# A graph network's edge loop: which engine fetches a sender's row, and the update's inputs

## The chip, the core and the metric

The kernel runs on one core of a Trainium2 chip. The core's engines run side by side, each on its own queue of instructions in the order given: TensorE (PE, with its weight loads PEld) multiplies matrices, VectorE (DVE) and ScalarE (ACT) work elementwise, GpSimd (POOL) issues the indirect gathers here, and SyncE (SP) issues most plain DMAs. ACT can issue DMAs too. The metric is the device time of one execution in microseconds. The kernel before takes 5600.84 us, the median of 12 runs (5595.15 to 5619.77).

## What is computed

There are 12,500 nodes of 64 features and 412,500 edges, sorted by receiver, each with 32 features. With h the layer norm of x, cut off at zero, each edge makes a message and an attention logit from its sender's row, its receiver's row and its own features. The softmax runs over all edges. The weighted messages are summed by receiver, and a small network makes the update that is added to x.

```python
h = jnp.maximum(_layernorm(x, axis=-1), 0.0)
msg_in = concat([h[src], h[dst], edge])            # 64 + 64 + 32
messages = swish(msg_in @ W1 + b1) @ W2 + b2
att = softmax(swish(msg_in @ Wa1 + ba1) @ Wa2 + ba2, axis=0)
aggregated = segment_sum(messages * att, dst)
x = x + swish(concat([h, aggregated]) @ Wu1 + bu1) @ Wu2 + bu2
```

Everything is float32.

## The kernel before

**The node stage.** The nodes are padded to 98 blocks of 128. Their normalized features h are made once, and kept transposed in SBUF as `hT`, two nodes to a column. Two tables are written to DRAM: `ts_d`, a row of 128 numbers for each node as a sender (h times the sender's part of Wa1 and W1), and `tr_d`, the same for the receiver with the biases. `hT_d` is a copy of `hT` in DRAM.

**The edge loop.** An edge tile is 125 edges (`EP`), one edge to a partition, and a group is 8 tiles (`K`); there are 413 groups (`NG`). `load(g)` brings a group's operands, two groups ahead of the group's own step (`AHEAD`). The senders' rows come from `ts_d` by indirect gathers on POOL, one for each tile, into one of the 7 buffers of the pool `gather` (L511 to L515). The gathers have 125 rows in even tiles and 126 in odd ones (`WIDE`); the last row of the 126 is not used. The receivers of a group lie in a window of 40 consecutive nodes (`W`), as two halves of 32, since the edges are sorted. Two DMAs on SP load the window's rows of `tr_d` (L534), at an address that SP reads from `base_sb`. Comparisons on DVE (L538) make a selection matrix from the edges' receivers, and one matrix product for each two tiles (L542) selects the receivers' rows and adds the edges' own features in one go. There are three window buffers (`WINS`), so a window's load waits for the product three groups before.

`begin(g)` adds the gathered rows to that product on DVE (L553) and takes tanh on ACT (L556). `end(g)` makes the messages and logits on DVE (L566 to L577); after its last read a gather buffer is free. Every fourth group the maximum is renewed and the exponentials are taken (L607, L610). `sum_up(g)`, some groups later, weighs the messages: DVE makes weight matrices (L620), PE sums by node (L626) and projects (L637), ACT copies between the two (L632), and DVE adds into `sums` at an address read from registers (L655, L658).

**Columns.** One group in three (`chosen`, `EVERY` and `PHASE`) doesn't gather its eighth tile. ACT copies the 125 senders' columns out of `hT` instead, one copy each at an address from a register (L484), with an address instruction ahead of each copy. The copies are issued in six lots of 24, 24, 24, 12, 24 and 17 (`SLOTS`), two lots at each step of the loop, one after `begin` and one after `end` (`burst`). The numbers of the senders come by a DMA on SP (`numbers`, L458), DVE turns them into columns (`places`, L467 to L473), a comparison picks the half (L547), and a product with `stack` adds the rows (L548); in `begin` a copy (L555) takes the place of the eighth add.

**The update's inputs.** Between the groups 17 and 120, the inputs of the update at the end are laid out in DRAM. `tile_bias`, in two steps for each of 13 node tiles, loads `hT_d` back from DRAM (L329), multiplies, copies on ACT (L348) and writes `bq_d`. `tile_rest` loads x, adds a bias on DVE and writes `xb_d`, all in one step. After the loop, 13 node tiles are finished from these.

**What sets the order.** `pin` keeps instructions in the program's order on their engine; a tile framework adds the waits that data and buffers need. DMAs of SP go round eight semaphores, and each waits until the one eight before it has landed. POOL's queue holds the gathers alone, so it runs ahead of the loop as far as the buffers allow.

Of the kernel before, what the change touches and what calls it, by code (L numbers as in the profile page):

```python
# [72 lines left out]

EVERY = 3
PHASE = 1
SLOTS = (((0, 24), (24, 24)), ((48, 24), (72, 12)), ((84, 24), (108, 17)))
ROUND = 12582912.0
WIDE = 126
EPS = 1e-5
# [4 lines left out]
PARTS = [("pair", 4 * C), ("we", C), ("bias", C), ("wu2h", 2 * D), ("wa2", U), ("bu2", D), ("w_bu", U),  # L84
         ("w2b", U), ("wu1a", U), ("wu2", D), ("ba2", 1)]
HALVED = 4
# [4 lines left out]
def gnn_kernel(ctx: ExitStack, tc: tile.TileContext, n_edges, x, src, src_row, dst, dst_row, first, edge,  # L91
# [33 lines left out]
    we, bias, wa2, bu2_r, ba2_c = (part[k] for k in ("we", "bias", "wa2", "bu2", "ba2"))  # L125
    w_bu = part["w_bu"][:D + 1]
    w2b = part["w2b"][:S1]
    wu1a, wu2 = part["wu1a"][:U], part["wu2"][:U]
# [32 lines left out]
    gather = ctx.enter_context(tc.tile_pool(name="gather", bufs=7))  # L161


    with tc.tile_pool(name="node1", bufs=1) as node1, \
# [40 lines left out]

        eps = node1.tile([P, 1], F32, name="eps")
        nc.vector.memset(eps, EPS)
# [127 lines left out]
def tile_bias(tc, c, first, v, work, ps, bus):  # L335

    nc = tc.nc
    m = min(NC, v["NB"] - c)
    if first:
        bus[c] = work.tile([U, P * NC], F32, name="bu", bufs=1)[:, :P * m]  # L340
    elif m <= 4:
        return
    i = 0 if first else 4
    n = min(4, m - i)
    pb = node_bias(tc, c + i, v, work, ps).rearrange("u b (h p) -> u h p b", h=2)
    to = bus[c].rearrange("u (h k p b) -> u k h p b", h=2, k=2, b=m // 2)
    for k in range(i // (m // 2), (i + n) // (m // 2)):
        nc.scalar.copy(to[:, k], pb[:, :, :, k * m // 2 - i:(k + 1) * m // 2 - i])  # L348
    if i + n == m:
        for h in range(2):  # L350
            nc.sync.dma_start(v["bq_d"][c // NC, h * U:(h + 1) * U, :P // 2 * m],
                              bus[c][:, h * P // 2 * m:(h + 1) * P // 2 * m])

# [5 lines left out]

def tile_rest(tc, c, v, work):  # L360

    nc = tc.nc
    n = min(NC, v["NB"] - c)
    xt = work.tile([P, 4, P], F32, name="hb").rearrange("p a b -> p (a b)")[:, :n * D]
    for k in range(2):
        nc.sync.dma_start(
            xt[k * P // 2:(k + 1) * P // 2].rearrange("p (h b d) -> p h b d", h=2, d=D),
            halves(v["x"], c, n, k, v["NB"]))
    xv = xt.rearrange("p (b d) -> p b d", d=D)
    nc.vector.tensor_tensor(xv, xv, v["bu2_r"][:, None, :].to_broadcast([P, n, D]), ALU.add)  # L370
    nc.sync.dma_start(v["xb_d"][c // NC, :, :n * D], xt)


def one_pass(tc, n_edges, v):
    nc = tc.nc
    NB, T, NG, NP, NT = (v[k] for k in ("NB", "T", "NG", "NP", "NT"))
    ident, iota_w, bj, dloc, src_full, base_sb, real, unreal, far, wrong = (
        v[k] for k in ("ident", "iota_w", "bj", "dloc", "src_full", "base_sb", "real", "unreal",
                       "far", "wrong"))
# [12 lines left out]
    with ExitStack() as ctx:  # L392
# [5 lines left out]
        stand = keep.tile([P, NH + 2 * W], F32, name="stand")  # L398
        base_lo = keep.tile([1, NG + 1], I32, name="base_lo")
        base_hi = keep.tile([1, NG + 1], I32, name="base_hi")  # L400
        nc.vector.memset(base_lo, 0)
# [34 lines left out]
        with tc.tile_pool(name="work2", bufs=2) as work2, \  # L436
                tc.tile_pool(name="small", bufs=3) as small, \
                tc.tile_pool(name="pre_ps", bufs=AHEAD + 1, space=PSUM) as pre_ps, \
                tc.tile_pool(name="one_ps", bufs=1, space=PSUM) as one_ps:
            pes, gss, lgs, ps_, psums, sps, pps, ees, mts, nums, cols = ({} for _ in range(11))  # L440

# [9 lines left out]

            chosen = {g for g in range(8, NG - 12) if g % EVERY == PHASE}

            def numbers(g):
                if g in chosen:
                    e = (g * K + K - 1) * EP
                    n = nums[g] = small.tile([P, EP], I32, name="num", bufs=2)
                    nc.sync.dma_start(n, bass.AP(tensor=v["src_row"].tensor,  # L458
                                                 offset=v["src_row"][:, e:].offset, ap=[[0, P], [1, EP]]))

            def places(g):
                if g not in chosen:
                    return
                n = nums[g]
                near = small.tile([1, EP], F32, name="near", bufs=1)
                to = small.tile([1, EP], I32, name="to", bufs=2)
                pin(nc.vector.tensor_scalar(to, n[0:1], 1, None, op0=ALU.logical_shift_right))  # L467
                m = NB // 2
                pin(nc.vector.tensor_scalar(near, to, 1.0 / m, 0.5 / m - 0.5, op0=ALU.mult, op1=ALU.add))
                pin(nc.vector.tensor_scalar(near, near, ROUND, None, op0=ALU.add))  # L470
                pin(nc.vector.tensor_scalar(near, near, ROUND, float(1 - m * P), op0=ALU.subtract, op1=ALU.mult))
                pin(nc.vector.scalar_tensor_tensor(to, to, float(P), near, op0=ALU.mult, op1=ALU.add))
                pin(nc.vector.tensor_scalar(n, n, 1, None, op0=ALU.bitwise_and))  # L473
                cols[g] = small.tile([P, EP], F32, name="cols", bufs=2), to

# [10 lines left out]
            def burst(g, k):  # L486
                for i in range(EVERY):
                    columns(g + 3 + i, *SLOTS[EVERY - 1 - i][k])

            at_sp, at_lo, at_hi, bus = {}, {}, {}, {}  # L490

# [4 lines left out]
            def registers(g, engine, at, base=base_sb, top=NP - 1):  # L496
# [4 lines left out]
                for i in range(n):  # L501
                    at[g + i] = regs[i]

            def load(g):

                t = g * K
                if g % NQ == 0:
                    registers(g, ENG.SP, at_sp)
                full = gather.tile([P, K, C], F32, name="gs")
                gs = gss[g] = full[:EP]  # L510
                for j in range(K - (g in chosen)):  # L511
                    rows = WIDE if j % 2 == 1 else EP
                    nc.gpsimd.indirect_dma_start(  # L513
                        out=full[:rows, j, :], out_offset=None, in_=ts_d[:, :],
                        in_offset=bass.IndirectOffsetOnAxis(ap=src_full[:rows, t + j:t + j + 1], axis=0))  # L515
                if g % NQ == 0:
# [16 lines left out]
                for r in range(2):  # L533
                    nc.sync.dma_start(win[r * R:(r + 1) * R, :, r, :],  # L534
                                      tr_w[bass.ds(at_sp[g], R), :, :])
                for h in range(2):
                    e = slice(h * E2 // 2, (h + 1) * E2 // 2)
                    pin(nc.vector.tensor_scalar(eo[:WR, e], db[:, e], bj[g // NQ % 2 * WR:(g // NQ % 2 + 1) * WR, g, h:h + 1], None,  # L538
                                                op0=ALU.is_equal))
                pe = pes[g] = pre_ps.tile([P, K, C], F32, name="pe")[:EP]  # L540
                for q in range(H):
                    pin(nc.tensor.matmul(pe[:, 2 * q:2 * q + 2, :], eo[:, q * EP:(q + 1) * EP],  # L542
                                         win[:, q // 2, :, :], start=True,
                                         stop=q < H - 1 or g not in chosen))
                if g in chosen:
# [4 lines left out]
            def begin(g):  # L550

                n = K - (g in chosen)
                pin(nc.vector.tensor_tensor(gss[g][:, :n, :], pes[g][:, :n, :], gss[g][:, :n, :], ALU.add))  # L553
                if n < K:
                    pin(nc.vector.tensor_copy(gss[g][:, n, :], pes[g][:, n, :]))  # L555
                pin(nc.scalar.activation(pes[g], gss[g], AF.Tanh))  # L556
# [161 lines left out]
            for g in range(NG):  # L718
# [18 lines left out]
                if g + AHEAD < NG:  # L737
                    load(g + AHEAD)
                numbers(g + EVERY + 4)
                places(g + EVERY + 3)  # L740
                if more:
# [20 lines left out]
                if g == min(40, NG):  # L762
                    pin(nc.vector.tensor_reduce(far[:, 1:2], dloc, AX.X, ALU.min, negate=True))
                if g == min(44, NG):

# [3 lines left out]
                    pin(nc.tensor.transpose(worst_ps, worst.to_broadcast([EP, EP]), ident[:EP, :EP]))  # L769
                if g == min(45, NG):  # L770
                    pin(nc.vector.tensor_reduce(worst, worst_ps, AX.X, ALU.max))
                    pin(nc.vector.tensor_scalar(wrong, worst, 0.0, None, op0=ALU.is_gt))
                if g >= 16 and g // 8 - 2 < NT:
                    c = (g // 8 - 2) * NC
                    if g % 8 in (1, 5):
                        tile_bias(tc, c, g % 8 == 1, v, work2, one_ps, bus)
                    elif g % 8 == 3:
                        tile_rest(tc, c, v, work2)

# [273 lines left out]
def _laid_out(w):  # L1053
# [16 lines left out]
    part["ba2"][:] = w["ba2"]  # L1070
    part["w_bu"][:D + 1] = np.concatenate([w["Wu1"][:D], w["bu1"][None]])
    part["w2b"][:S1] = np.concatenate([w["W2"], w["b2"][None]])
    part["wu1a"][:U] = w["Wu1"][D:]
# [42 lines left out]
```

## Time and profile before

| | |
|---|---|
| median of 12 runs | 5600.84 us |
| the profiled execution, its time | 5631.02 us |
| its span, first to last instruction | 5629.3 us |
| mean granted TensorE clock | 0.597 |
| first gather starts, last ends | 52.1 us, 5522.7 us |
| first tanh, last tanh (L556) | 101.2 us, 5577.8 us |
| busy: DVE, ACT, POOL, PE | 59%, 44%, 63%, 46% |

The profile is one execution. A group of instructions is given as: line, engine, operation, output and inputs, count, then busy time in us and mean duration of one in ns, then the idle time of the engine just before them and what ended most of it. "issue" stands for idle time in which the engine waited for nothing that the profile shows. Register and address instructions and the issuing of DMAs are not counted as busy. A name with a q (SPq) means the engine's sequencer. In the windows view each engine has its busy time and the number of instructions in that stretch. In the timeline a row is: start, duration, engine, line, operation, count, and in brackets the idle time before it and what ended it.

### The profile page before, as it was taken

How to read it: one execution, taken by the hardware profiler on the slowest of the kernel's cores; microseconds unless marked ns; L12 is line 12 of the kernel's file. 1: busy time of each engine (PE TensorE's matmuls, PEld its weight loads, DVE VectorE, ACT ScalarE, POOL GpSimd, SP SyncE). 2: the span in 40 equal slices, each digit the busy share in tenths (PEclk: the TensorE clock that was granted, in tenths of full speed). 3: DMA queues.
4: the chain of work that ended last, by engine and by line, in shares of the span. 5: the costliest groups of instructions: out<-in, count | busy, mean ns of one | idle time of the engine just before them, and what ended most of it. 6: DMA issues, size and time to landing. Idle time of an engine off the chain costs nothing. (4 is left out here: it accounts for less than half of the span.)

```text
span 5629.3 us, 81803 instructions
## 1 busy us (share of the span) xinstructions
PE 2567.6 (46%) x11509; PEld 2001.9 (36%) x11509; DVE 3347.3 (59%) x9768; ACT 2485.4 (44%) x17651; POOL 3538.5 (63%) x3198
## 2 busy tenths in 40 slices
PE   5244544444444444444444444444444444444446
PEld 4233333333333333333333333333333333333335
DVE  6365656656656555555555555565656555555557
ACT  3344444444444444444444444444444444444422
POOL 4666666666666666666666666666666666666662
PEclk8565656666656555555555565566565555555556
DMA  7233333233232222222222222222222222222232
GB/s 227 61 73 70 76 78 76 69 80 77 71 71 65 62 63 68 58 66 61 65 65 63 64 67 59 65 62 66 66 62 64 68 58 65 60 66 65 62 82 68
DMA packets 335625, 398.57 MB, mean 71 GB/s; under 512 B 170293, under 2 KB 266088, under 8 KB 334690
## 3 DMA queue, kind: packets, MB, share of 16 engines
q0 software_dynamic: 205168, 205.98, 15.6%
q1 hardware_dynamic: 128530, 177.64, 13.1%
q10 hardware_dynamic: 1376, 9.67, 0.4%
q14 instruction: 457, 3.74, 0.2%
q8 instruction: 94, 1.54, 0.1%
HBM read 365.34 MB, written 25.72 MB: 69 GB/s over the span
## 5 line engine op out<-in xcount | busy, mean ns | idle before, releaser
L513 POOL DMA_INDIRECT gs<-ts_d,src_sb x3173 | 3521.2, 1110 | 1999.1 <-issue 1886.4
L484 ACT COPY cols<-hT 128x1 f32 x16375 | 1900.4, 188 | 2523.3 <-issue 2440.6
L542 PE MATMUL pe<-wins,eo 128*125 128x256 f32 x3304 | 1507.6, 634 | 863.9 <-DVE lg L577 257.3
L542 PEld LDWEIGHTS pe<-wins,eo 128*125 128x125 f32 x3304 | 1001.1, 319 | 1195.5 <-DVE lg L577 296.8
L637 PE MATMUL mt<-ss,w2u 65*128 65x40 f32 x826 | 225.1, 369 | 1305.4 <-DVE gm L603 583.1
L620 DVE TENSOR_SCALAR wt<-iota_w,dloc,p 125x40 f32<-125x40 f32 x3304 | 748.8, 333 | 1.6
L626 PE MATMUL sp<-wt,acts 125*65 125x40 f32 x6608 | 719.4, 286 | 17.1 <-issue 14.1
L637 PEld LDWEIGHTS mt<-ss,w2u 65*128 65x128 f32 x826 | 208.8, 296 | 1454.1 <-issue 822.2
L626 PEld LDWEIGHTS sp<-wt,acts 125*65 125x65 f32 x6608 | 682.2, 205 | 23.9 <-issue 17.0
L566 DVE SCALAR_TENSOR_TENSOR acts<-pe,gs 125x512 f32<-125x512 f32 x413 | 284.6, 689 | 560.2 <-ACT pe L556 438.8
L553 DVE TENSOR_TENSOR gs<-pe,gs 125x1024 f32<-125x1024 f32 (+1 forms) x413 | 486.5, 1178 | 182.6 <-remote 119.2
L556 ACT ACTIVATE pe<-gs 125x1024 f32<-125x1024 f32 x413 | 422.6, 1023 | 344.5 <-DMA gs<-ts_d,src_sb 101.8
L655 DVE TENSOR_TENSOR sums<-sums,mt 64x40 f32 x606 | 115.7, 191 | 511.5 <-remote 482.6
L596 PE MATMUL mt<-ident,mx 125*128 125x125 f32 x110 | 48.1, 437 | 591.8 <-DVE sums L655 251.7
L538 DVE TENSOR_SCALAR eo<-dbs,bj 64x250 f32<-64x250 int32 x826 | 289.7, 378 | 18.2 <-DMA dbs<-in_dst_row_dram 8.7
L574 DVE TENSOR_TENSOR pe<-pe,w_all 125x512 f32<-125x512 f32 x413 | 288.8, 699 | 13.4
L572 DVE SCALAR_TENSOR_TENSOR pe<-pe,gs 125x512 f32<-125x512 f32 x413 | 286.9, 695 | 9.2
L577 DVE TENSOR_REDUCE lg<-pe 125x8 f32<-125x512 f32 x413 | 283.8, 687 | 9.5
L547 DVE SCALAR_TENSOR_TENSOR cols<-num,half,cols 128x125 f32<-128x125 int32 x131 | 45.7, 349 | 367.0 <-ACT cols L484 298.8
L596 PEld LDWEIGHTS mt<-ident,mx 125*128 125x128 f32 x110 | 20.0, 182 | 603.3 <-remote 434.0
L691 DVE SCALAR_TENSOR_TENSOR total<-total,scale,psum 125x1 f32<-125x1 f32 x110 | 23.5, 214 | 297.1 <-ACT p L610 274.8
L548 PE MATMUL pe<-stack,cols 128*125 128x128 f32 x262 | 78.3, 393 | 208.9 <-DVE cols L547 122.1
(125 smaller groups left out, 1207.9 us busy)
## 6 DMA issues: line engine op xcount, KB each, us to landing
eo<-in_edge_dram SPq DMA_DIRECT2D x103, 500.0 KB
dbs<-in_dst_row_dram SPq DMA_DIRECT2D x206, 250.0 KB
gs<-ts_d,src_sb POOLq DMA_INDIRECT x3173
wins<-tr_d SPq DMA_DIRECT2D x826, 32.0 KB
num<-in_src_row_dram SPq DMA_DIRECT2D x131, 62.5 KB
ts_d<-ts SPq DMA_DIRECT2D x5, 896.0 KB
tr_d<-tr ACTq DMA_DIRECT2D x5, 896.0 KB
hT_d<-hT ACTq DMA_DIRECT2D x1, 3136.0 KB
```

What stands on the lines that cost most here:

```text
L484: pin(nc.scalar.copy(to[:, first + i:first + i + 1], hT[:, bass.ds(regs[i], 1)]))
L513: nc.gpsimd.indirect_dma_start(out=full[:rows, j, :], out_offset=None, in_=ts_d[:, :], in_offset=bass.IndirectOffsetOnAxis(ap=src_full[:ro ...
L538: pin(nc.vector.tensor_scalar(eo[:WR, e], db[:, e], bj[g // NQ % 2 * WR:(g // NQ % 2 + 1) * WR, g, h:h + 1], None, op0=ALU.is_equal))
L542: pin(nc.tensor.matmul(pe[:, 2 * q:2 * q + 2, :], eo[:, q * EP:(q + 1) * EP], win[:, q // 2, :, :], start=True, stop=q < H - 1 or g not in ...
L553: pin(nc.vector.tensor_tensor(gss[g][:, :n, :], pes[g][:, :n, :], gss[g][:, :n, :], ALU.add))
L556: pin(nc.scalar.activation(pes[g], gss[g], AF.Tanh))
L566: pin(nc.vector.scalar_tensor_tensor(acts[g % ACTS][:, :, 0:U], th[:, :, U:C], 1.0, gs[:, :, U:C], op0=ALU.add, op1=ALU.mult))
L572: pin(nc.vector.scalar_tensor_tensor(att, th[:, :, 0:U], 1.0, gs[:, :, 0:U], op0=ALU.add, op1=ALU.mult))
L574: pin(nc.vector.tensor_tensor(att, att, wa2[:EP, None, :].to_broadcast([EP, K, U]), ALU.mult))
L620: pin(nc.vector.tensor_scalar(wt[:, j, :], iota_w[:EP, j // H, :], dloc[:, g * K + j:g * K + j + 1], p[:, k + j:k + j + 1], op0=ALU.is_equ ...
L626: pin(nc.tensor.matmul(sp, acts[g % ACTS][:, j, :], wt[:, j, :], start=j == 0, stop=j == K - 1))
L637: pin(nc.tensor.matmul(pp, w2u.rearrange("s h u -> s (h u)"), sps.pop(g), start=True, stop=True))
```

## The change

There are five parts.

- All gathers have 125 rows; `WIDE` goes.
- Columns are copied in two groups of five, at g mod 5 = 1 and 4, in five lots of 24, 24, 24, 24 and 29, two lots at each step.
- In each eighth group from 8 to 408, one more tile (the last, or the last but one where the last is made of columns) is not gathered on POOL. SP loads its 125 rows of `ts_d` by 125 DMAs of one row, 16 at each of the eight steps before, at addresses read from registers, into a tile of its own (`alone`). `begin` adds that tile by itself.
- `tile_bias` multiplies from `hT` in SBUF, two nodes to a column, with block-diagonal weights, adds the bias on DVE instead of by an extra row, and writes to DRAM two steps later. `tile_rest` is spread over three steps.
- For the first four groups, rows of x itself are gathered, before `ts_d` exists. `features` normalizes them on the edges, transposes them, and a further product multiplies them by the sender's weights.

```diff
-EVERY = 3
-PHASE = 1
-SLOTS = (((0, 24), (24, 24)), ((48, 24), (72, 12)), ((84, 24), (108, 17)))
+LOTS = ((0, 24), (24, 24), (48, 24), (72, 24), (96, EP - 96))
+ROUNDS = 5
+SLOTS = {1: ((5, 1), (4, 0), (4, 1), (3, 0), (3, 1)), 4: ((5, 0), (5, 1), (4, 0), (4, 1), (3, 0))}
 ROUND = 12582912.0
-WIDE = 126
+QUEUES = [(ENG.SP, 8, 0, 16)]
+RAW = 4
...
+    raw_src = const.tile([P, RAW * K], I32, name="raw_src")
+    nc.scalar.dma_start(raw_src, src[:, :RAW * K])
+    raws = [gather.tile([P, K, C], F32, name="gs") for _ in range(RAW)]
+    for g in range(RAW):
+        for j in range(K):
+            nc.gpsimd.indirect_dma_start(
+                out=raws[g].rearrange("p k c -> p (k c)")[:EP, j * D:(j + 1) * D], out_offset=None, in_=x[:, :],
+                in_offset=bass.IndirectOffsetOnAxis(ap=raw_src[:EP, g * K + j:g * K + j + 1], axis=0))
...
-    pb = node_bias(tc, c + i, v, work, ps).rearrange("u b (h p) -> u h p b", h=2)
+    pb = ps.tile([P, 4, P], F32, name="mt")[:, :n // 2, :]
+    pin(nc.tensor.matmul(pb, v["w_bup"], v["hT"][:, (c + i) // 2:(c + i + n) // 2, :], start=True, stop=True))
     to = bus[c].rearrange("u (h k p b) -> u k h p b", h=2, k=2, b=m // 2)
-    for k in range(i // (m // 2), (i + n) // (m // 2)):
-        nc.scalar.copy(to[:, k], pb[:, :, :, k * m // 2 - i:(k + 1) * m // 2 - i])
...
+        pin(nc.vector.tensor_scalar(
+            to[:, k, :, :, at:at + 2 * q - 1:2],
+            pb[rows, (b - i) // 2:(b - i) // 2 + q, :].rearrange("u q (h p) -> u h p q", h=2),
+            v["bu1"][rows], None, op0=ALU.add))
...
-            chosen = {g for g in range(8, NG - 12) if g % EVERY == PHASE}
+            chosen = {g for g in range(8, NG - 12) if g % ROUNDS in SLOTS}
...
             def burst(g, k):
-                for i in range(EVERY):
-                    columns(g + 3 + i, *SLOTS[EVERY - 1 - i][k])
...
+                for i in (3, 4, 5):
+                    slots = SLOTS.get((g + i) % ROUNDS, ())
+                    if (i, k) in slots:
+                        columns(g + i, *LOTS[slots.index((i, k))])
...
+            def rows(q, g):
+                engine, every, phase, n_rows = QUEUES[q]
...
+                a = at * n_rows
+                n = min(n_rows, EP - a)
+                if n <= 0:
+                    return
+                loads, regs = nc.values_load_multi_w_load_instructions(
+                    rows_at[q, g][0:1, a:a + n], engines=[engine], min_val=0, max_val=NP - 1,
+                    skip_runtime_bounds_check_because=WHY)
+                for one in loads:
+                    pin(one)
+                for k in range(n):
+                    pin(dma[engine].dma_start(alone[g][a + k:a + k + 1, :], ts_d[bass.ds(regs[k], 1), :]))
...
+            def features(g):
+
+                gs = gss[g] = v["raws"][g][:EP]
+                xg, xm = (gs[:, h * H:(h + 1) * H, :].rearrange("p k (r d) -> p (k r) d", d=D) for h in range(2))
+                total = small.tile([EP, K], F32, name="raw_t", bufs=1)
+                pin(nc.vector.tensor_reduce(total, xg, AX.X, ALU.add))
+                pin(nc.vector.scalar_tensor_tensor(xm, total[:, :, None].to_broadcast([EP, K, D]), -1.0 / D, xg,
+                                                   op0=ALU.mult, op1=ALU.add))
+                pin(nc.scalar.activation(xg, xm, AF.Square))
...
+                pin(nc.scalar.activation(rstd, rstd, AF.Sqrt, bias=v["eps"][:EP], scale=1.0 / D))
+                pin(nc.vector.reciprocal(rstd, rstd))
...
+                for q in range(H):
+                    pin(nc.tensor.transpose(pt[:, q, :], xg[:, 2 * q:2 * q + 2, :], ident[:EP, :EP]))
+                to = raw_to[g] = v["raws"][g][:, H:, :EP]
+                pin(nc.scalar.copy(to, pt))
...
-                full = gather.tile([P, K, C], F32, name="gs")
-                gs = gss[g] = full[:EP]
-                for j in range(K - (g in chosen)):
-                    rows = WIDE if j % 2 == 1 else EP
+                if g < RAW:
+                    features(g)
+                else:
+                    gss[g] = gather.tile([P, K, C], F32, name="gs")[:EP]
+                gs = gss[g]
+                for j in range(0 if g < RAW else K - (g in chosen) - (g in alone)):
                     nc.gpsimd.indirect_dma_start(
-                        out=full[:rows, j, :], out_offset=None, in_=ts_d[:, :],
-                        in_offset=bass.IndirectOffsetOnAxis(ap=src_full[:rows, t + j:t + j + 1], axis=0))
+                        out=gs[:, j, :], out_offset=None, in_=ts_d[:, :],
+                        in_offset=bass.IndirectOffsetOnAxis(ap=src_sb[:, t + j:t + j + 1], axis=0))
...
+                if g in alone:
+                    pin(nc.vector.tensor_tensor(gss[g][:, n, :], pes[g][:, n, :], alone.pop(g), ALU.add))
...
-                numbers(g + EVERY + 4)
-                places(g + EVERY + 3)
+                numbers(g + 7)
+                places(g + 6)
...
-                if g == min(44, NG):
+                if g == min(46, NG):
```

## The prediction

> **What bounds the kernel now.** I read the page's groups first, then the groups' waits on ACT, then stretches of the timeline in the steady loop, then windows by stage. The chain that ended last is of no use here: it covers the last 0.1 us only.
>
> ```profile
> PE 2567.6 (46%) x11509; PEld 2001.9 (36%) x11509; DVE 3347.3 (59%) x9768; ACT 2485.4 (44%) x17651; POOL 3538.5 (63%) x3198
> ...
> L513 POOL DMA_INDIRECT gs<-ts_d,src_sb x3173 | 3521.2, 1110 | 1999.1 <-issue 1886.4
> L484 ACT COPY cols<-hT 128x1 f32 x16375 | 1900.4, 188 | 2523.3 <-issue 2440.6
> ...
> L556 ACT ACTIVATE pe<-gs 125x1024 f32<-125x1024 f32 x413 | 422.6, 1023 | 344.5 <-DMA gs<-ts_d,src_sb 101.8
> ```
>
> No engine is over 63% busy, yet two groups fill their engines if idle time is added. The one-column copies of L484 hold ACT for 1900.4 + 2523.3 = 4424 us, 0.270 us each, and 2440.6 us of that is "issue": ACT waits for nobody. With tanh (L556, 422.6 + 344.5) that is 5191 of the 5477 us from the first tanh to the last. POOL's gathers take 1.11 us and 0.30 us between two: 3173 x 1.41 = 4474 us; the other 1000 us it stands still. The groups' tanh follows POOL's last gather of the same group by 65 to 86 us (median 76), five to six groups, so POOL waits for a free buffer and not the consumer for data.
>
> How a copy's price comes about shows in the timeline around one of POOL's pauses (POOL gathers without a gap from 2502.7 to 2523.7 and rests until 2529.9):
>
> ```profile
> 2516.24 0.28 ACT L484 COPY cols<-hT 128x1 f32 x2 [1.16 <-issue]
> 2517.67 0.19 ACT L484 COPY cols<-hT 128x1 f32 x1 [1.14 <-issue]
> 2518.05 0.19 ACT L484 COPY cols<-hT 128x1 f32 x1 [0.19 <-issue]
> 2519.76 0.28 ACT L484 COPY cols<-hT 128x1 f32 x2 [1.52 <-issue]
> ...
> 2524.87 0.65 ACT L484 COPY cols<-hT 128x1 f32 x6 [1.02 <-issue]
> ...
> 2527.41 2.32 ACT L484 COPY cols<-hT 128x1 f32 x24 [0.61 <-issue]
> ```
>
> While POOL gathers, two copies take some 1.4 us; in the pause 24 take 2.32 us, 0.097 each. I sorted all copies by whether a gather was running when they started, and took the time to the next copy: 11,399 under gathers at 0.316 us, 4,975 in pauses at 0.175 us (4465 us together, in keeping with the 4424 above). Under gathers the price grows with the length of the stretch: 0.13 to 0.24 us in its first 8 us, 0.37 from 8 to 12, 0.52 to 0.55 until 24, 0.68 beyond. Where POOL does not pause at all, from 145 to 216 us, ACT gets 58 copies done in 71 us:
>
> ```profile
> 145.00:216.00 71.00, 6.16 (x26) 4.76 (x26) 7.29 (x19) 10.84 (x60) 52.05 (x48) 0.52 0.25 58
> ```
>
> (the columns are window, length, then busy time and count of PE, PEld, DVE, ACT, POOL, then clock, DMA share, GB/s). ACT spent nearly all of it in copies. So ACT bounds the loop, POOL's running sets its speed, and POOL's pauses are the time in which ACT catches up. From 1000 to 5000 us POOL issues 2302 gathers, 300 groups of 7.667: a group takes 13.32 us, of which 7.667 x 1.405 = 10.77 are gathers. ACT's copies take 41.67 x 0.273 = 11.38 of it, the rest of ACT 1.94.
>
> **The change part by part.**
>
> *Gathers of 125 rows.* Now odd tiles gather 126 rows. The trace has two durations in turn, 1.21 us (125 rows, first of each group) and 1.00 us (126). Afterwards all are 1.21 + 0.30 = 1.51 us.
>
> *Columns in two groups of five.* 157 groups of 8 to 400 instead of 131: 19,625 copies instead of 16,375, that is 49.94 a group instead of 41.67, and 26 gathers fewer. Loads of ACT's registers stay at five or six a chosen group, 785 in all as now. DVE gets 26 more sets of L467 to L473, L547 and L555, some 2.1 us each: 55 us over the run. DVE is at 8.1 us a group and hidden by ACT.
>
> *Rows on SyncE.* In 51 groups (8, 16, ... 408) one tile leaves POOL, 51 gathers fewer, and comes as 125 one-row DMAs from SP, 16 at each step: 6,375 DMAs, each with an address instruction. The nearest row is the pair of window loads of L534, from the end of one to the end of the next: 0.52 us in pauses, 0.70 us under gathers, 0.63 on average.
>
> ```profile
> L534 SPq MOVE wins<-tr_d x826: 3/29/729, 83.3 to 5536.2; - x166
> L534 SPq DMA_DIRECT2D wins<-tr_d x826: 5/317/1892, 83.3 to 5536.3; - x166
> ```
>
> Sixteen rows take 16 x 0.63 = 10.1 us a group; two window loads 1.2 and the remaining loads some 0.9 make 12.2 us of SP. That is under 15 us (below), so I put it at nothing, hidden by ACT. Queued behind the rows are the next window loads, for which PE waits; they are issued 31 us ahead of their matmuls now (median; 25 at the 5% mark), which covers one burst of rows. Bounds: 0.52 us a row gives 10.4 us a group; if a row's three instructions go the way of ACT's at their worst, 0.71 us for two, a row takes 1.07 and SP 19.2 us a group. The maximum of 729 ns on a MOVE says that SP knows the stall. In `begin`, 51 extra adds of 125x128 cost DVE at most 0.28 us each (L555's row): 14 us, hidden.
>
> *Both together in the steady loop.* Gathers a group: 8 - 0.400 - 0.130 = 7.47, x 1.51 = 11.28 us. ACT has T - 1.94 us for copies, of which the share 11.28/T runs under gathers at 0.316 us and the rest at 0.175:
>
> 49.94 = (T - 1.94) x (11.28/T / 0.316 + (1 - 11.28/T) / 0.175), so T = 15.07 us.
>
> The same equation with 41.67 copies and 10.77 us gives 13.3, the present period. 393 groups x (15.07 - 13.32) = +688 us. Bounds: all extra copies at 0.097 us give 8.27 x 0.097 x 393 = +315; at the 0.68 us of long stretches +2210. I take the two measured averages, since the mix of stretches and pauses stays what it is.
>
> *Update's bias from SBUF.* Goes: 50 loads hb<-hT_d with the SP waits on them (70 us), 26 ACT copies of L348 (14 us and 30 us idle before them). Comes: some 50 DVE operations of about 0.35 us (nearest: a 64x250 comparison, L538, 0.378), 18 us, hidden. Worth what ACT saves: -15 us; between 0 and -45. The x and output-side loads of `tile_rest` are the same DMAs spread over three steps; the check's shift by two groups moves three small operations. Nothing, ACT covers them.
>
> *First four groups from input rows.* 32 gathers run from about 10 to 60 us, while POOL now waits for the table until 52 us. Now POOL works without a pause from 52 to 211 us, and in the tail of that the loop crawls: tanh of groups 4 to 9 takes from 122 to 242 us, where six periods would be 80. Four groups fewer to gather take up to 4 x 11.3 = 45 us from that stretch. Against it stand, for groups 2 and 3 in the loop, a chain DVE-ACT-DVE-ACT-DVE-PE-ACT of some 8 us each and four activation table loads of 1.28 us. Net -20 us; bounds -60 and +30.
>
> Sum against the profiled execution (5631.0 us, span 5629.3): 5631 + 688 - 15 - 20 = 6284. The median of the runs is 5600.8, 30 us lower, so 6254; I say 6260.
>
> One rule speaks the other way. The Trainium skill, "Runtime: NRT & Kernel Launch", section "Instruction fetch mechanics", says that a sequencer streams a long program ahead and that fetching is mostly hidden. If the "issue" stalls are fetches, this trace differs: 2440.6 us of them on one line. By the page every copy would take its 0.097 us, ACT would need 6.8 us a group, and POOL's 11.28 us would set the end at some 4760 us; I keep to the rows.
>
> **The rivals.** (1) SP becomes the bound. For: stalls of 0.7 us on its MOVEs, and more than five times as many instructions on its queue. Against: 12.2 us by the mean row. It decides from (15.07 - 2.1) / 16 = 0.81 us a row; at 0.9 us T is 16.5 and the time 6820, at 1.07 us 19.2 and 7890. (2) Faster: the stalls thin out. The copies now come evenly, two lots at each step, and after every wait ACT runs its first 15 or so copies fast even under gathers; all gathers change their form too. It decides where the mean copy falls under (13.32 - 1.94) / 49.94 = 0.228 us, from 0.273; at 0.20 us T is 11.9 and the time 5020. Against: at the stalled places the stalls per us are alike under both forms of gather (0.9 to 1.1 a us, by where the cycle is cut), and POOL's longer gathers lengthen the stretches. (3) The extra copies are had cheaply, at 0.097 to 0.15 us, because most fall into pauses: 5600 + 315 to 490 - 35, so 5880 to 6055. (4) No change within 0.2% (about what a measurement of this kernel can tell): only if gain and loss cancel.
>
> **How the numbers follow.** The forecast (6080 to 6500) has 0.50, rival 1 0.22, rival 3 0.15, rival 2 0.11, rival 4 0.02. So faster 0.11, same 0.02, slower 0.87. The range runs from 5850 to 6950: below it lies rival 2, above it the dear half of rival 1, some 0.19 in all.
>
> **What would show it.** Right: L484's successor with 19,625 copies at 0.26 to 0.29 us including idle time; gathers of one duration, 1.21 us; about 265 gathers in 550 us (7.47 in 15 us); POOL pausing over 3 us a group; window loads still well ahead of their matmuls. Wrong: PE or DVE waiting on window loads, with SP never waiting for PE (rival 1); copies under 0.228 us and POOL without pauses (rival 2). The start is right if the ninth group's tanh comes some 20 us earlier than now, relative to the first.

## The result, and the profile after

The changed kernel takes 5777.43 us (median of 9 runs, 5762.54 to 5798.11) beside 5599.57 us before: a ratio of 1.0319, 95% interval 1.0305 to 1.0333. It is slower, as forecast, but by 178 us and not by 660. Its profiled execution has a span of 5819.4 us.

The groups of the page, after (in the page's order):

```profile
PE 2458.8 (42%) x11609; PEld 1995.3 (34%) x11609; DVE 3462.9 (60%) x10072; ACT 2786.5 (48%) x20891; POOL 3771.1 (65%) x3121
...
L608 POOL DMA_INDIRECT gs<-ts_d,src_sb x3064 | 3709.0, 1211 | 1951.8 <-issue 1849.5
L514 ACT COPY cols<-hT 128x1 f32 x19625 | 2194.6, 187 | 2129.3 <-issue 2046.1
L640 PE MATMUL pe<-wins,eo 128*125 128x256 f32 x3304 | 1526.0, 641 | 2605.6 <-DMA wins<-tr_d 2034.6
```

L514 is the old L484. There are 3250 more copies, yet ACT spends less on them: 2194.6 + 2129.3 = 4324 us, 0.220 us each, where before took 4424 us at 0.270. POOL still stands still, and a wait is new: PE stops before the product of a group (L640, the old L542) until its windows have been loaded. In before most of its idle time ended otherwise:

```profile
L542 PE MATMUL pe<-wins,eo 128*125 128x256 f32 x3304 | 1507.6, 634 | 863.9 <-DVE lg L577 257.3
```

The waits view of after's profiled execution (waiting engine and line, what for, us, times, longest):

```profile
PE pe L640 <- DMA wins<-tr_d: 2034.6, 288, 16.6
...
DVE to L497 <- DMA num<-in_src_row_dram: 751.7, 117, 14.5
```

Both are loads issued by SP. The window loads are now issued 2.6 us ahead of their matmul (median), where it was 31 us. The timeline of after shows the new queue and ACT's new pace together:

```profile
3004.28 14.99 SPq L558 DMA_DIRECT2D one_gs<-ts_d  x16
...
3005.09 0.28 ACT L514 COPY cols<-hT 128x1 f32 x2 [0.47 <-issue]
3005.85 0.28 ACT L514 COPY cols<-hT 128x1 f32 x2 [0.47 <-issue]
...
3020.80 0.77 SPq L629 DMA_DIRECT2D wins<-tr_d  x2
...
3024.67 1.61 PE L640 MATMUL pe<-wins,eo 128*125 128x256 f32 x3 [8.55 <-DMA wins<-tr_d]
```

Sixteen one-row DMAs hold SP for 15 us; two window loads follow 1.5 us later, and PE, 8.55 us idle, starts when they have landed. ACT does two copies in 0.75 us while POOL gathers; in before's lines it was two in about 1.4 us. So ACT stalls less, and SP seems to have become the engine that sets the period (the runs below test this): 13.83 us a group between the tanh of groups 20 and 400 (before 13.31).

### The profile page after: what moved, and what is told of

Its sections match the earlier page's. It is cut to its first block, busy times and chain, and to the rows that moved or that the text cites. A ratio compares the mean times of both kernels' runs of the same rounds, so it can differ in the third digit from the quotient of the medians.

```text
span 5819.4 us, 108561 instructions
## 1 busy us (share of the span) xinstructions
PE 2458.8 (42%) x11609; PEld 1995.3 (34%) x11609; DVE 3462.9 (60%) x10072; ACT 2786.5 (48%) x20891; POOL 3771.1 (65%) x3121
## 3 DMA queue, kind: packets, MB, share of 16 engines
q1 hardware_dynamic: 138054, 179.47, 13.8%
## 5 line engine op out<-in xcount | busy, mean ns | idle before, releaser
L608 POOL DMA_INDIRECT gs<-ts_d,src_sb x3064 | 3709.0, 1211 | 1951.8 <-issue 1849.5
L514 ACT COPY cols<-hT 128x1 f32 x19625 | 2194.6, 187 | 2129.3 <-issue 2046.1
L640 PE MATMUL pe<-wins,eo 128*125 128x256 f32 x3304 | 1526.0, 641 | 2605.6 <-DMA wins<-tr_d 2034.6
L640 PEld LDWEIGHTS pe<-wins,eo 128*125 128x125 f32 x3304 | 1019.6, 324 | 2901.6 <-issue 1692.7
L732 PE MATMUL sp<-wt,acts 125*65 125x40 f32 x6608 | 652.3, 271 | 30.0 <-DVE wt L726 29.5
L732 PEld LDWEIGHTS sp<-wt,acts 125*65 125x65 f32 x6608 | 616.5, 187 | 36.4 <-DVE wt L726 31.4
L497 DVE TENSOR_SCALAR to<-num 1x125 int32<-1x125 int32 x157 | 42.7, 272 | 791.2 <-DMA num<-in_src_row_dram 751.7
L657 DVE TENSOR_TENSOR gs<-pe,gs 125x1024 f32<-125x1024 f32 (+2 forms) x409 | 471.2, 1152 | 34.7 <-issue 12.1
L743 PE MATMUL mt<-ss,w2u 65*128 65x40 f32 x826 | 194.7, 330 | 356.7 <-DVE gm L709 132.6
L680 DVE TENSOR_TENSOR pe<-pe,w_all 125x512 f32<-125x512 f32 x413 | 288.8, 699 | 13.8
L764 DVE COPY stand<-nmax 64x40 f32 x826 | 186.0, 225 | 3.6 <-issue 0.3
L738 ACT COPY ss<-sp 65x40 f32<-65x40 f32 x413 | 75.5, 183 | 150.8 <-remote 93.4
```

Source lines behind the costliest of these rows:

```text
L514: pin(nc.scalar.copy(to[:, first + i:first + i + 1], hT[:, bass.ds(regs[i], 1)]))
L608: nc.gpsimd.indirect_dma_start(out=gs[:, j, :], out_offset=None, in_=ts_d[:, :], in_offset=bass.IndirectOffsetOnAxis(ap=src_sb[:, t + j:t ...
L680: pin(nc.vector.tensor_tensor(att, att, wa2[:EP, None, :].to_broadcast([EP, K, U]), ALU.mult))
L732: pin(nc.tensor.matmul(sp, acts[g % ACTS][:, j, :], wt[:, j, :], start=j == 0, stop=j == K - 1))
L743: pin(nc.tensor.matmul(pp, w2u.rearrange("s h u -> s (h u)"), sps.pop(g), start=True, stop=True))
```

## The experiments

Each lot of runs has its own runs of before beside it, on the same chip, and all ratios are to those. The lots ran on different chips. I call them A (lots 1 and 2, before at 5572 and 5587 us), B (lot 3, before at 4605 us), C (lot 4, 5630 us) and D (lot 5, 5398 us). The chip of the result above (before at 5599.57 us) is not on record, and of before there is one profile, that of the front of this document. That before itself differs by a fifth between them became a result of its own.

Two theories for the cheap copies: F, that the form of the gather sets ACT's stalls; W, that ACT's copies are cheap only because ACT now waits for SP and spreads them. And S: that SP's rows set the period after.

### Lot 1, chip A: one part at a time

**All gathers at 125 rows, nothing else.**

```diff
-WIDE = 126
+WIDE = 125
```

> The kernel before with one edit: odd tiles gather 125 rows too; 131 chosen groups, no rows on SP, old start. Theory F (the form of the gather sets how much ACT is stalled: after, with 125-row gathers alone, a copy in a long stretch of gathers takes 0.26 to 0.31 us, where before it took 0.52 to 0.68): the mean copy falls from 0.270 us to 0.20 to 0.23 including idle time, the period to 11.3 x to 12 us, the time to 5000 to 5250 us, although each gather takes 1.21 us. Theory W (ACT's copies are cheaper after only because ACT waits for window loads and its queue refills meanwhile): the mean copy stays at 0.26 to 0.28 us, POOL gathers 0.8 us longer a group, the time is 5600 to 5800 us.

Measured: 4954.51 us, ratio 0.890 (0.8868 to 0.8932). Its page:

```profile
L513 POOL DMA_INDIRECT gs<-ts_d,src_sb x3173 | 3851.0, 1214 | 1034.4 <-issue 938.3
L484 ACT COPY cols<-hT 128x1 f32 x16375 | 1863.4, 187 | 1784.0 <-issue 1733.9
```

Without any rows on SP the same 16,375 copies cost 0.223 us. F holds and W falls. POOL pauses for 21 us in all (1043 before): though each odd gather takes 0.21 us more of POOL, the kernel gains 11%, because ACT no longer holds POOL back.

**After without the rows on SP.**

```diff
-QUEUES = [(ENG.SP, 8, 0, 16)]
+QUEUES = []
```

> The kernel after without the rows on SyncE: all tiles that are not made of columns are gathered on POOL, 3115 gathers. Theory S (the rows on SP bound the loop after: window loads come late, PE waits 2034 us for them): that wait goes to under 100 us, and the time falls. By theory F a copy stays at 0.20 to 0.24 us, ACT needs 1.94 + 49.94 x 0.22 = 12.9 us a group, the time is 5350 to 5500 us. By theory W ACT becomes the bound again and a copy goes back to 0.27 us: 15.1 us a group, 6200 to 6350 us. If SP is no bound at all: 5750 to 5800 us.

Measured: 4986.57 us, ratio 0.894 (0.8906 to 0.8975). The wait on window loads is gone:

```profile
L514 ACT COPY cols<-hT 128x1 f32 x19625 | 2165.0, 187 | 1853.6 <-issue 1751.5
L640 PE MATMUL pe<-wins,eo 128*125 128x256 f32 x3304 | 1522.0, 638 | 726.9 <-DVE eo L636 259.8
```

S holds: between this ratio and after's 1.032 lie 13.8% of before, some 770 us, which the rows on SP cost; the whole change loses a quarter of that. It came out lower than expected, since the copies became cheaper still (0.205 us).

**After with its odd tiles gathered at 126 rows again.**

```diff
+                    wide = 126 if j % 2 == 1 else EP
                     nc.gpsimd.indirect_dma_start(
-                        out=gs[:, j, :], ...
+                        out=full[:wide, j, :], ...
```

> The kernel after with odd tiles gathered with 126 rows as before; all else as after. Theory F: ACT's and SP's stalls grow again: a copy goes from 0.220 to 0.26 to 0.29 us, a row on SP from 0.66 to 0.8 us and more, and the time rises to 6100 to 6500 us, although POOL's gathers take 0.8 us less a group. Theory W: POOL's shorter gathers leave longer pauses, 5650 to 5780 us.

Measured: 6416.2 us, ratio 1.152 (1.1476 to 1.1561). With the old form kept, the rest of the change loses about what I had forecast, and more, but not by the forecast's path: a copy costs 0.239 us, under F's 0.26 to 0.29, and it is PE that waits longer still for windows, a row on SP now taking 0.74 us.

```profile
L514 ACT COPY cols<-hT 128x1 f32 x19625 | 2186.4, 187 | 2503.8 <-issue 2423.6
L642 PE MATMUL pe<-wins,eo 128*125 128x256 f32 x3304 | 1523.8, 639 | 3140.2 <-DMA wins<-tr_d 2511.6
```

**Before without any columns.**

```diff
-            chosen = {g for g in range(8, NG - 12) if g % EVERY == PHASE}
+            chosen = set()
```

> The kernel before without any columns: every tile is gathered on POOL, 3304 gathers, ACT has no one-column copies. If ACT's copies bound the kernel before, as the prediction read it, POOL is the next bound: 8 x 1.405 = 11.24 us a group, no pauses, 413 x 11.24 + 110 us of start and end = 4750 us. If something else that the columns hide bounds the loop at 13.3 us (DVE, PE, the buffers), the time is 5500 us or more.

Measured: 5206.78 us, ratio 0.934 (0.9311 to 0.9377), a period of 12.26 us. I had expected POOL's own 11.3; POOL still pauses for 413 us, so something besides the copies holds it back too.

### Lot 2, chip A: the form of the gather, and fewer rows

**No columns, all gathers at 125 rows** (both edits above).

> Before without any column copies and with all gathers at 125 rows; the 131 tiles that went through columns are gathered again, so the result is the same. Theory F (the 126-row gathers cost time only through the stalls they put between ACT's copies): with no copies left the form of the gather no longer matters much. POOL then issues 8 gathers a group at 1.21 + 0.30 us = 12.1 us, 413 groups 4990 us, and with the 163 us of start and end that the run with all gathers at 125 rows leaves over its own 7.68 gathers a group, 5150 us: about 1% below the 5207 us of before without columns and with 126 rows. Rival G (126-row gathers slow everything, copies or none): 5207 times 0.89, 4630 us, which would need gathers shorter than the 1.51 us seen.

Measured: 5126.79 us, ratio 0.919 (0.9161 to 0.921), period 12.12 us, which is 8 x 1.51 of POOL; it pauses for 5 us. The form that gains 11% with the copies gains 1.6% without them. So the larger part of its effect goes through ACT's copies, but not all: with them POOL's pauses fell by 1022 us, and without them they still fall by 408, of which the dearer gathers take back 342. What held POOL back there is not separated; SP, too, stalls less (of its 1,654 register and move operations 140 took over 0.4 us in the run before, 16 in this one).

**After with 126-row odd tiles and without rows**: columns, bias and start, under the old form.

> After with its odd tiles gathered at 126 rows again, and without the one-row DMAs on SP (those tiles are gathered by POOL). The forecast's own sum, which put all its growth on ACT: 47.5 copies a group at 0.27 us and the rest give 15.1 us a group, 6150 to 6260 us. Theory F with the price that the run with rows and 126 showed (0.239 us a copy, 11.4 us, and 2.6 us of other ACT work): 14.0 us a group, 5850 to 5950 us. Rival W (the rows on SP alone made that run slow): 5000 to 5300 us, like the run without rows at 125 rows.

Measured: 5812.62 us, ratio 1.042 (1.0387 to 1.0443). That is just under F's range. The forecast's term was too large even here: 0.245 us a copy.

**Before with every gather at 126 rows**, not every second one.

```diff
-                    rows = WIDE if j % 2 == 1 else EP
+                    rows = WIDE
```

> Before with every gather at 126 rows instead of every second one. Theory F as a dose (the more 126-row gathers, the dearer each copy): 0.223 us a copy with none, 0.270 us with half of them, so 0.30 to 0.32 us with all, 39.65 copies a group, 12.0 to 12.7 us and 2.6 us of other ACT work: 14.5 to 15.3 us, 6150 to 6450 us. Rival M (it is the change of form from gather to gather that costs, not the 126 rows): copies at 0.22 us or less, POOL at 7.68 gathers of 1.00 + 0.30 us, 10 us a group, ACT 11.3 us, 4800 to 4950 us.

Measured: 5968.43 us, ratio 1.071 (1.066 to 1.075). A shorter gather (1000 ns) and a slower kernel:

```profile
L513 POOL DMA_INDIRECT gs<-ts_d,src_sb x3173 | 3172.4, 1000 | 2680.6 <-issue 2543.6
L484 ACT COPY cols<-hT 128x1 f32 x16375 | 1875.9, 188 | 2871.4 <-issue 2832.7
```

0.290 us a copy: M falls (it is not the alternation), and F's dose is there, though smaller than I wrote. With none, half and all of the gathers at 126 rows a copy costs 0.223, 0.270 and 0.290 us.

**After with half of the rows on SP.**

```diff
-QUEUES = [(ENG.SP, 8, 0, 16)]
+QUEUES = [(ENG.SP, 16, 0, 8)]
```

> After with half of the one-row DMAs: one tile in 16 groups, 8 rows a group. Theory S (the rows cost only where SP's own time exceeds the period): SP has 8 rows at 0.66 us, 5.3 us, and 3.1 us of other work, 8.4 us a group, under POOL's 7.54 gathers at 1.51 us, 11.4 us: 4880 to 4990 us, no slower than without rows (4987 us). Rival P (every row costs in proportion, through DMA traffic or stalls): halfway between 4987 and 5777 us, 5380 us.

Measured: 5171.53 us, ratio 0.927 (0.9238 to 0.9292): between the two, so neither S in this strict form nor P holds. The windows are 30 us ahead again, and PE no longer waits for them, so SP does not bind; but a copy costs 0.212 us where it was 0.205, and POOL's pauses grew from 185 to 403 us. Half of the rows cost 3.2% of before without SP being full; the other half, which fills SP, 10.5%.

### Lot 3, chip B: before takes 4605 us

**Before with fixed columns**, to see whether reading a register is what stalls.

```diff
-                    pin(nc.scalar.copy(to[:, first + i:first + i + 1], hT[:, bass.ds(regs[i], 1)]))
+                    pin(nc.scalar.copy(to[:, first + i:first + i + 1], hT[:, first + i:first + i + 1]))
```

> Before with each one-column copy reading a fixed column in place of the one that its register names; the registers are still loaded, but the register operation ahead of each copy (16375 of them, 1763 us of ACT's idle time in before, 1309 us of it in 1856 that take about 0.7 us) is gone. This leaves out the choice of the column, so these tiles' receivers are wrong; the work is otherwise the same. Theory I (ACT's instruction stream stalls now and then, about once in so many instructions, while POOL gathers): half of the instructions, so half of the 1309 us: ACT 650 us and the 454 us of normal register time shorter, until POOL's own 7.68 gathers at 1.41 us and its waits bind: 5000 to 5250 us. Theory T (it stalls once in so much time, whatever it runs): the stalls move into the idle time ahead of the copies: 5400 to 5600 us. Theory R (only reading a register stalls): loads left alone, 5000 us or less, and no idle of about 0.7 us ahead of a copy.

Measured: 4605.06 us, ratio 1.000 (0.9991 to 1.001). The register loads went as well, since nothing reads them.

**Every gather at 128 rows** (`rows = WIDE`, `WIDE = 128`):

> Before with every gather at 128 rows (three rows past a tile's 125 are fetched and not used). Theory F by form (what matters is how a gather is spread, and 125 is the mild form): copies at 0.29 to 0.31 us as with 126 rows throughout, ACT bound, 5900 to 6250 us. Rival A (126 alone is the bad form): copies at 0.22 to 0.24 us, 4900 to 5350 us.

Measured: 4093.03 us, ratio 0.889 (0.8875 to 0.8902). Neither run answers its question here, and the reason shows in the register operation ahead of each copy: first before as profiled ahead of the prediction, on another chip, then the 128-row run on B (the source view, whose three numbers are shortest, median and longest in ns).

```profile
L484 ACTq FUSED_REGOPS  x16375: 2/37/1602, 126.4 to 5423.3; - x200
```

```profile
L484 ACTq FUSED_REGOPS  x16375: 37/37/43, 124.3 to 3884.4; - x200
```

And the copies of the same run, from its page:

```profile
L484 ACT COPY cols<-hT 128x1 f32 x16375 | 1617.9, 187 | 752.5 <-issue 737.7
```

On B not one of them stalls, even under 128-row gathers; a copy costs 0.145 us, ACT is far from the bound, and POOL pauses for 2 us in all. Then POOL's gathers alone set the time: 3173 x (1.11 + 0.30) = 4474 us and the ends make before's 4605, and 0.947 us for a 128-row gather makes the 4093.

**After without rows and without the raw start**, then **after without rows and with columns in one of three** (`ROUNDS = 3` with before's lots):

> After without the one-row DMAs and without the start from gathered input rows (the first four groups gather normalized rows, as in before); the rest as in after without rows, 4987 us. The forecast gave this start 20 us: 5000 to 5010 us. If it is hidden or cancelled by what it adds ahead of the first groups (first activation at 106 against 101 us, group 20 at 379 against 383 us): 4980 to 4995 us.

> After without rows and with columns in one group of three, in the lots of before, in place of two of five: against before with all gathers at 125 rows (4955 us) it differs by the bias and the start alone, which the forecast put at -35 us: 4920 us. Against after without rows (4987 us) it shows the columns alone under 125-row gathers: 65 fewer column groups and tiles' copies on ACT, 26 more gathers on POOL at 1.51 us, +39 us if POOL binds (5025 us); less than 4987 us if ACT's copies still cost more than the gathers that they save.

Measured: 4890.28 us, ratio 1.062 (1.0604 to 1.0633), and 4903.44 us, ratio 1.065 (1.0633 to 1.0662). After without rows gains 11% on A; on B these two near relatives of it lose 6%: a 125-row gather is 0.21 us dearer than a 126-row one to POOL, and here POOL binds. The two differ in the start and in the columns. The run with the new start is 23 us ahead at group 20's tanh (282.3 against 305.1 us), though not at the ninth (170.1 against 166.5 us). The other has columns in two of five, which shorten the period from 11.64 to 11.53 us, 44 us from group 20 to group 400.

### Lot 4, chip C: the same again

> After, unchanged, beside before once more, because before itself took 4605 us in the last lot and 5572 to 5587 us in the lots ahead of it. If before takes about 5600 us here: 5750 to 5800 us again. If it takes about 4600 us (no stalls of about 0.7 us in ACT's stream): SP's rows at the 0.45 us that they take in POOL's pauses, 15.4 a group, 6.9 us, and 3.1 us of other work, 10 us, under POOL's 7.42 gathers at 1.51 us, 11.2 us: POOL binds, 4770 us, ratio 1.035. Rival: the rows take 0.74 us under gathers there too, SP 14.5 us a group: 5800 us or more.

> Before with all gathers at 125 rows again. If before takes about 5600 us here: 4955 us, ratio 0.89. If about 4600 us: POOL bound with 3173 gathers at 1.21 + 0.30 us: 4920 to 4940 us, ratio 1.07: the same edit a gain on the one chip and a loss on the other.

> Before with all gathers at 128 rows again. If before takes about 4600 us here: 4093 us, ratio 0.889. If about 5600 us: theory F by form says copies at 0.29 to 0.31 us as with 126 rows throughout (5968 us), 5900 to 6250 us; if instead 128 is mild, copies at 0.22 to 0.24 us, 4900 to 5350 us.

> Before with fixed columns again (leaves out the choice of the column; the register operations are gone, and the loads with them, since nothing reads them). If before takes about 4600 us here: no difference, as measured, since POOL binds. If about 5600 us: ACT's stream is one instruction a copy. Theory I (a stall comes once in so many instructions): with a third to a half of the instructions left, copies at 0.12 + 0.04 us, POOL's 10.8 us a group and its waits bind: 4650 to 5250 us. Theory T (a stall comes once in so much time while POOL gathers, whatever ACT runs): the stalls move ahead of the copies, 0.24 us or more a copy, 5300 to 5600 us.

Before took 5630 us, so the stalls were back. After: 5819.78 us, ratio 1.033 (1.0286 to 1.0364). All at 125: 5008.16 us, 0.890 (0.8869 to 0.8933). All at 128: 6141.9 us, 1.090 (1.0866 to 1.0938). Fixed columns: 5218.64 us, 0.928 (0.9248 to 0.9303). First the copies of the 128-row run, then those of the run with fixed columns:

```profile
L484 ACT COPY cols<-hT 128x1 f32 x16375 | 1856.5, 187 | 3075.0 <-issue 3014.1
```

```profile
L484 ACT COPY cols<-hT 128x1 f32<-128x1 f32 x16375 | 1800.2, 189 | 1322.5 <-issue 1289.1
```

The one edit to 128 rows gives 0.889 on B and 1.090 on C. There a copy costs 0.301 us under it, the dearest of the forms. Fixed columns cost 0.191 us and still stall, so R falls: a stream of ACT's instructions without register operations stalls too. Without stalls (B) the two streams cost 0.145 and 0.095 us a copy, so the stalls add 0.125 us (46% of the time) with the register operation and 0.096 us (50%) without. Nearly equal shares speak for T, though my figure for T (0.24 us or more) did not allow for the shorter copy; but I's 0.16 us is not far off, and the time, 5219 us, lies in the range that I had for I (4650 to 5250) and not in T's (5300 to 5600). This is not decided.

### Lot 5, chip D: after and before nearly level

> After, unchanged. Where before takes about 5600 us: 5780 to 5820 us, ratio 1.032, as twice before. Where before takes about 4605 us (ACT's stream without stalls): POOL binds with 7.42 gathers a group at 1.51 us, 11.2 us, SP's rows at 0.45 us take 6.9 us of it: 4770 us, ratio 1.035; with rows at 0.74 us SP binds, 5800 us or more.

> After without rows and with columns in one group of three, as before has them: all that is left of the change is the 125-row gathers, the bias and the start. Where before takes about 5600 us: 35 us under before with all gathers at 125 rows (ratio 0.89) by the forecast's terms for bias and start, ratio 0.884; if they bring nothing, 0.89; if the two in five columns of after without rows (ratio 0.894) cost nothing against one in three, they all agree within 0.5%. Where before takes about 4605 us: 4903 us, ratio 1.065, as measured.

Measured: after 5360.32 us beside before's 5398.1, ratio 0.9937 (0.9908 to 0.9966); without rows and with columns in one of three 4902.03 us, ratio 0.908 (0.9068 to 0.9094). Before's time on D lies between those of B and C. Under 125-row gathers without the rows only 55 of 16,375 register operations took over 0.4 us, and the time is that of B. In after 934 of 19,625 did, so on D most of these stalls came with the rows on SP or the columns in two of five, which no run there separates, and not with the 125-row gathers alone. PE waits for windows on D too:

```profile
L514 ACT COPY cols<-hT 128x1 f32 x19625 | 2092.1, 187 | 1632.3 <-issue 1526.1
L640 PE MATMUL pe<-wins,eo 128*125 128x256 f32 x3304 | 1515.6, 636 | 2292.6 <-DMA wins<-tr_d 1747.3
```

## Why the prediction was right in sign by luck, and wrong in size

In shares of before: columns, bias and start +4.2%; the 125-row form on top of them -14.7%; the rows on SP +13.8%. The first two steps were measured on chip A, and the third leads to after's own ratio, 1.032, so that the three add up to it by construction. They depend on the order: with the form first, it brings -11.0%, and columns, bias and start then +0.4%, which is not clear of the intervals (0.890 and 0.894). The forecast had +12% for columns, bias and start and nothing for the other two. So the sign was luck: the term it rested on was worth at most 4.2 of its 12%, and two terms that it put at nothing nearly cancel. The 5777 us lie below its whole range (5850 to 6950) and in the range of none of its rivals.

- *The bound before.* Right on A: with the copies left as they are and only the form of the gathers changed, they stall less and the kernel gains 11%. Not on B, where POOL binds.
- *Gathers of 125 rows.* This is the first of two steps that failed. It was costed for POOL alone (1.51 us each), and 0.316 us under gathers was carried over, with the sentence that "the stalls per us are alike under both forms of gather". Before's trace mixed the two forms in turn, one every 1.4 us, and ACT's stalls last 0.7 us and may run past a gather's end, which is probably why it did not tell them apart. Cut in the same way, after has 0.237 us under gathers and 0.144 in pauses. The forecast's equation with these two gives T = 12.9 us, not 15.07: 0.4 us less than before a group, 160 us in all, a faster kernel. These prices come from after itself, so the equation is only shown to follow them; the run without rows on SP is the test, and its period is 11.84 us.
- *Columns.* Oversized even under the old form: +226 us together with bias and start, where the equation gives 14.8 us a group, some +555 after the -35 for those two. That the copies now come evenly may be why; no run separates it.
- *Rows on SyncE.* The second step that failed. Costed at nothing, hidden by ACT, they cost 13.8% of before (11.0% with odd tiles at 126, 1.152 against 1.042); the cover was the 15.07 us that never came. The price of a row was near: 0.66 us (0.74 under gathers, 0.45 in pauses) for 0.63. What was left out is the reading of the row numbers into SP's registers (L552), 372 us between 400 and 5300 us, 1.05 us a group; with the window loads' 1.6 us, SP has some 13.4 of the 13.83 us filled. Rival 1 had its mechanism right, but its point of decision, 0.81 us a row, hung on T = 15.07. At T = 12.9 it falls to (12.9 - 2.1) / 16 = 0.68 us, and with the 3.2 us that SP's other work measured to 0.61.
- *Rivals 1 and 2 came true together, each in part.* Mean copy 0.220 us, under rival 2's 0.228, though POOL still pauses for some 1080 us; PE waiting for windows, rival 1's sign. Each was weighed as if the other kept to the forecast.
- *Bias.* Not separated by any run; its 50 DVE operations (L367) take 24 us. *Start.* -20 forecast, to be seen in the ninth tanh relative to the first. In after that distance is 109.2 us and not 123.5, the change in stalls included; on chip B, where nothing stalls, it is 64.9 us with the new start and 66.9 without, and the 23 us show only by group 20, with other columns beside them. The start's worth is not shown.
- *Instruction fetch.* The Trainium skill, "Runtime: NRT & Kernel Launch", section "Instruction fetch mechanics", holds fetching to be mostly hidden. On chips A, C and D the copies stall all the same; on B they do not, and without rows and without the new start the kernel takes 4890 us there, near the 4760 us that the page's picture had given. That the stalls are fetches is not shown, and the profile speaks against one packet of instructions for each stall. Its table of DMA queues has this line (packets, MB, share of 16 engines) in before, and then in the 128-row run on B:

```profile
q14 instruction: 457, 3.74, 0.2%
q14 instruction: 457, 3.74, 0.3%
```

With the 94 packets of a second such queue that is 551 for all engines in either run, while ACT alone had 1,856 register operations over 0.4 us in the first and none in the second.

## What to carry to other kernels

A price read under a mixture of two forms may not be carried to a kernel that has only one: run the uniform form first, both ways, since it is one line. When a cheap term lets the period fall, work out anew from where the next engine binds, and count the loading of addresses into registers in what a queue gets. And measure on more than one chip before a change of a few per cent is called a gain or a loss: this one went from 1.033 to 0.994.

## What the runs showed of the hardware

- While POOL issues indirect gathers, instructions of ACT and of SP can stall by about 0.7 us at a time. In before 1,856 of ACT's 16,375 register operations took over 0.4 us, 1,803 of them begun while POOL gathered and the others within 3 us after; on SP it was 111 of 1,654, on DVE none of 1,652. How much goes with the rows in a gather: per copy, POOL's pauses included, 0.223 us under 125 rows, 0.290 under 126, 0.301 under 128 (chips A and C). For POOL and the landing the order is the reverse: 1.21, 1.00 and 0.95 us to issue, and 3.2, 2.4 and 2.3 us from the start of the issue to landing. The Trainium skill, "DMA: Bandwidth & Descriptors", section "Why a DMA increments its semaphore by 16 and not by 1", has the number of DMA engines from the largest divisor up to 16 of the row count: 5, 14 and 16 for these. The traces agree: a gather's rows move as 15 packets of 4096 bytes and 5 of 512, as 14 and 14, and as 16 and none, which are 5 shares of 25 rows, 14 of 9 and 16 of 8. The order of all three measures goes with it; that the engines in use are what slows ACT is not shown.
- The same kernel took 4605 us on one chip and 5398 to 5630 us on three others. Before itself was not profiled on B; its variants there show none of these stalls (in the 128-row run all 16,375 register operations lay between 37 and 43 ns), and POOL's gathers alone come to its time, so the stalls account for the difference as far as the record goes. B's granted TensorE clock was higher too, 0.63 for before against 0.59 on C. What sets B apart, the chip or something that ran or lay in memory beside it, stays open.
- All gathers at 125 rows was not the fastest form on every chip, but the steadiest: 4955 and 5008 us on A and C, and 4902 and 4903 us, with the new bias and start, on D and B, against 4605 to 5630 us before. On a chip without stalls, 128 rows are better, at 4093 us.
